# Attention's projections set ahead by a step or two, the feed-forward's weight preparation taken into attention, and a conditional pass put first

## The chip, the cores and the metric

The kernel runs on one core of a Trainium2 chip, as one program that is launched once. Five engines each work through a queue of their own, in order: PE (matrix multiplication, with PEld for its weight loads), DVE (vector), ACT (scalar functions), POOL (GpSimd) and SP (which here only starts DMAs). The metric is the device time of one execution in microseconds (us); four runs of the kernel before are given, and their median is what a time of the kernel after is held against.

## The reference

A two-layer block on 64 sequences of 64 tokens with 256 channels, 4096 tokens in all, in f32. Only the first layer's attention and feed-forward bear on the change:

```python
x = x + attn(cond(x, cond_1024), query_proj, key_proj, value_proj, output_proj)
x = x + ffn(cond2(x, cond_1024, weight), norm1_w, w1, act_scale, act_bias, norm2_w, w2)
# ... second layer: recurrent net, state-space scan, two mixtures of experts

def attn(x, ...):                  # 16 heads, keys of 16, values of 64
    q, k, v = x @ query_proj, x @ key_proj, x @ value_proj
    a = softmax(q k / sqrt(16), axis=1)
    return (a v) @ output_proj

def cond2(x, y, weight):           # y: one row for each sequence
    ys = y / sqrt(256)
    d = rsqrt((ys * ys) @ (weight * weight) + EPS)
    return (x * ys[:, None, :]) @ weight * d[:, None, :]

def weight_quant(w):               # in both products of ffn
    scale = 1.0 / clip(mean(abs(w)), 1e-5, None)
    return clip(round(w * scale), -1, 1) / scale
```

The feed-forward quantizes its activations too (root mean square, largest absolute value, rounding to 127 steps) and has relu squared between its two products. The conditioning `cond` ends with a projection whose bias is `bo`; in the data of this case `bo` is zero.

## The kernel before

**Stages.** The program goes through its stages one behind the other: a convolution and scan that make `cs`, what attention reads (`conditioned_scan`, L129, until about 146 us); `attention` (L301, to 431.6 us); `ffn0` (L486, to about 700 us); `rnn`, `mamba` with the first mixture beside it, and `mixtures`. The feed-forward's weights are loaded behind the scan (`ffn0_weights`, L449); further down SP's queue follow large fills of memory for the mixtures (`regions`) and copies of weights (`packed`), which keep the DMA engines busy from 100 to 340 us. The residual `xT` stays in the fast memory, with the channels on the partitions.

**Attention.** Rather than project values and outputs apart, the kernel multiplies `cs` as it stands by the attention weights and then by `M`, which is Wv times Wout, made by `value_weights` (L288: four times PE L297 into a bank, evicted by DVE). `keys` is `cs` transposed, 128 tokens by 128 (PE L317, evicted in turn by DVE and ACT).

`attend` (L330) goes over eight units (`NU`) of 512 tokens. A unit has four steps, (i, h) = (0,0), (0,1), (1,0), (1,1), here called A, B, C and D; a letter with a stroke (A') is a step's work done later. Each step has four parts:

- `scores`: eight matrix products q k on PE, each of several passes (L385), into two PSUM banks; for each bank DVE takes the maximum (L390) and subtracts it (L391); ACT takes exp of 128x1024 (L397); DVE the row sums z (L400) and their reciprocals; POOL multiplies E by them (L401).
- `follow`: a list, `late`, holds back the rest of a step until two more steps have been issued. Then `values` gives E times `keys` (PE L410) into two banks, which ACT copies to `oT` (L412).
- behind the fourth step's `values` `project_out` follows: two times eight products of 128x512 (L418) and an addition to `xT` on DVE (L420).
- `project_in(u+1)`, issued behind step D's scores: for q and then for k four products on PE (L359) into two banks, and their evictions, all on ACT: 16 for q (L367: masked by head and biased, 128x256) and four for k (L364).

PSUM has eight banks in two rings: "acc" (4) for `values`, `project_out`, M and keys; "ps" (4) for scores, q and k, which is why a product into a "ps" bank waits for the eviction of what was written four banks before. The scheduler builds each engine's queue from the order of issue and what each instruction waits for; so the first q and k, M and the keys are set beside the tail of the scan.

**The bias pass.** Where `bo` is not zero the same `attend` runs once more with a vector of biases in place of values. A count of nonzero entries, `wa.any`, is loaded into a register of each engine (L321) and a branch (L322) jumps over it, as it does with this data. It stands behind the main `attend`.

**The feed-forward's preparation.** `ffn0` begins with what depends on weights alone: `ternary` (L469) for w1 and w2 (a reduction of the absolute values L475, their sum over partitions by PE L477, the mean L478, its reciprocal L479, two passes over 128x2048, L480 and L481, and a cast, L482), a factor L506 for each, and for the conditioning `ys`, `ysq`, `wsq` (L509 to L513), four passes of a product (PE L516) and `rsqrt` (L89: a square root on ACT, then five DVE instructions L92 to L96). Then a software pipeline goes over 16 pairs of tiles of 128 tokens; its first stage, `product`, is xs on POOL (L562), PE L573 and L577, dt on ACT (L579) and gm on DVE (L580).

Of the kernel before, what the change touches and what calls it, by code (L numbers as in the profile page):

```python
# [300 lines left out]
def attention(g, wa, cs):  # L301
# [4 lines left out]
    nc, tc = g.nc, g.tc  # L306
    with tc.tile_pool(name="keys", bufs=1) as kp:
        M = kp.tile([P, wa.H // 2, D], F32, name="M")
        rows = kp.tile([P, NT // CH, 2, P], F32, name="keys")
        cs2 = cs.rearrange("p b l -> p (b l)")  # L310

        def before():
            value_weights(g, wa, lambda i, r: wa.Wv[r, i, :], M)
# [6 lines left out]
        attend(g, wa, cs2, lambda u, i: rows[:, u, i], M, before)  # L320
        for v in nc.values_load_multi_w_load_instructions(wa.any, min_val=0, max_val=D)[1]:  # L321
            with tc.If(v > 0):  # L322
                ones = kp.tile([P, P], F32, name="ones")
                nc.vector.memset(ones, 1.0)
                c = kp.tile([P, wa.H // 2, D], F32, name="c")
                bv = lambda i, r: wa.bv[r, i : i + 1].to_broadcast([L, L])
                attend(g, wa, cs2, lambda u, i: ones, c, lambda: value_weights(g, wa, bv, c, 1.0 / L))


def attend(g, wa, cs2, keys, M, before):  # L330
# [12 lines left out]
    with (  # L343
# [4 lines left out]
        def project_in(u):  # L348
# [5 lines left out]
            for i in range(2):  # L354
                ps = [bank(g, (P, 2, UT)) for _ in range(2)]
                for hg in range(2):
                    for h in range(2):
                        W = wa.Wqkv[half(h), i * HK + hg * P : i * HK + (hg + 1) * P]
                        nc.tensor.matmul(ps[h][:, hg, :], W, cs2[half(h), ts(u, UT)], start=True, stop=True)  # L359
                for h in range(2):  # L360
                    for hg in range(2):
                        if i:
                            b = wa.bqk[:, 1, hg : hg + 1]
                            nc.scalar.activation(v.k[:, hg, h, :], ps[h][:, hg, :], AF.Identity, bias=b)  # L364
                        else:
                            for j in range(4):
                                nc.scalar.activation(  # L367
                                    v.q[:, hg, h, :, j, :],
# [63 lines left out]
        for u in range(NU):  # L432
            for i in range(2):
                for h in range(2):
                    late.append((u, now, h, i, scores(now, h, i)))
                    if not (u or i or h):
                        before()
                    if i and h and u + 1 < NU:
                        now = project_in(u + 1)
                    if len(late) > 2:  # L440
                        follow()
# [1591 lines left out]
```

## Time and profile before

| what | us |
|---|---|
| four runs | 2945.47, 2947.01, 2947.2, 2950.5 |
| their median | 2947.11 |
| the profiled execution | 2955.37 |
| its span, first to last instruction | 2953.7 |
| attention's starts of L418, one for each unit | 183.27, 217.30, 251.24, 284.99, 318.39, 351.64, 385.78, 414.71 |
| attention's last addition to xT | 430.91, for 0.69 |
| the feed-forward's first gm | 456.31 |

Busy times over the whole span, and the first slices of 73.8 us each (a digit is the busy share in tenths; attention lies in slices 3 to 6, the feed-forward in 6 to 10):

```profile
PE 2421.3 (82%) x12134; PEld 1719.5 (58%) x12148; DVE 1756.8 (59%) x2955; ACT 1406.2 (48%) x2402; POOL 1306.2 (44%) x1117
## 2 busy tenths in 40 slices
PE   4978866778957788888787888868987899999996
PEld 4533323446824455555555565646875678888885
DVE  0454447884059997989887979895244343333232
ACT  0564435775366576767555666653422222222220
```

Read them thus: no engine is busy all the way, so the limits differ from stage to stage. In attention (third to sixth digit) PE has 6 to 8 tenths, ACT 3 to 6, DVE 4 to 5: something waits for something in each unit. How the rest is to be read (stretches, timelines, chains of waits) is told where it is used.

### The profile page before, as it was taken

Reading aid. Unit: us, or ns where it says so; the run is one execution under the profiler, and the core shown is the slowest. Engines: PE = TensorE matmul, PEld = TensorE weight load, DVE = VectorE, ACT = ScalarE, POOL = GpSimd, SP = SyncE. Lnnn points to the kernel's source line nnn. Section 1 sums busy time; section 2 is a strip of 40 time slices with the busy share of each in tenths; the row PEclk is TensorE's granted clock in tenths of the full one; section 3 lists DMA queues with packets and bytes.
Section 4 is the critical chain, followed back from the end, with each engine's and each line's share of the span. In section 5 each row is a group of like instructions: output and inputs, shape, how many; then the busy total and the mean of one; then the engine's idle time right before and its main releaser. Section 6 shows DMA issues by size and latency. Waiting matters only on the chain.

```text
span 2953.7 us, 34689 instructions
## 1 busy us (share of the span) xinstructions
PE 2421.3 (82%) x12134; PEld 1719.5 (58%) x12148; DVE 1756.8 (59%) x2955; ACT 1406.2 (48%) x2402; POOL 1306.2 (44%) x1117
## 2 busy tenths in 40 slices
PE   4978866778957788888787888868987899999996
PEld 4533323446824455555555565646875678888885
DVE  0454447884059997989887979895244343333232
ACT  0564435775366576767555666653422222222220
POOL 0022214552056767677757777773644441111110
PEclk9989987889767898999889999989998999999998
DMA  9999611000011222221212212222686856555655
GB/s 235 370 356 340 195 29 42 19 19 19 15 50 58 86 69 68 69 75 62 75 44 68 90 68 90 77 96 74 208 265 225 309 204 245 207 211 187 220 182 180
DMA packets 183075, 406.04 MB, mean 137 GB/s; under 512 B 25312, under 2 KB 89056, under 8 KB 177520
## 3 DMA queue, kind: packets, MB, share of 16 engines
q1 hardware_dynamic: 169456, 366.80, 37.0%
q0 software_dynamic: 13440, 36.98, 3.2%
q8 instruction: 97, 1.59, 0.2%
q14 instruction: 82, 0.67, 0.1%
HBM read 280.76 MB, written 144.98 MB: 144 GB/s over the span
## 4 chain that ended last, share of the span: by engine, by line
PE 43%; DVE 20%; ACT 9%; issue 6%; POOL 4%; DMA 2%; SPq 0%; DVEq 0%; ACTq 0%; POOLq 0%
DVE hb L954 11%; PE ps L1540 11%; PE acc L1438 8%; DVE hb L956 3%; PE ps L1507 2%; PE yp L970 2%; PE mq L1676 2%; PE mq L1692 2%; DVE xc L796 2%; PE mp L851 2%; PE ps L690 1%; PE ps L573 1%; POOL hb L915 1%; PE acc L690 1%; PE mp L789 1%
## 5 line engine op out<-in xcount | busy, mean ns | idle before, releaser
L915 POOL TENSOR_TENSOR hb<-dx,Bn 128x1024 f32<-128x1024 f32 x256 | 601.1, 2357 | 261.9 <-PE yp L970 256.0
L954 DVE TENSOR_TENSOR_SCAN hb<-dA,hb 128x512 f32<-128x512 f32 x512 | 602.9, 1209 | 32.5 <-ACT dA L922 29.9
L922 ACT ACTIVATE dA<-delta,A 128x504 f32<-128x504 f32 x512 | 344.3, 683 | 305.6 <-DVE hb L954 302.4
L970 PEld LDWEIGHTS yp<-ident,hb 128*128 128x128 f32 x2048 | 268.4, 152 | 180.6 <-issue 142.2
L956 DVE TENSOR_TENSOR hb<-hb,cb 128x1024 f32<-128x1024 f32 x256 | 312.1, 1219 | 83.0 <-PE cb L867 66.2
L1540 PE MATMUL ps<-gxT,w 128*128 128x256 f32 (+1 forms) x1600 | 325.9, 362 | 0.8 <-DVE gxT L1415 0.8
L1540 PEld LDWEIGHTS ps<-gxT,w 128*128 128x128 f32 x1600 | 277.1, 191 | 47.2 <-issue 12.1
L970 PE MATMUL yp<-ident,hb 128*128 128x128 f32 x2048 | 302.7, 292 | 0.0
L1676 PE MATMUL mq<-x,moe_s 128*128 128x256 f32 x896 | 250.4, 412 | 49.1 <-ACT up L1683 28.4
L1222 POOL DMA_INDIRECT ffn_y<-gy,to x72 | 69.3, 962 | 457.9 <-ACT gy L1440 445.9
L1676 PEld LDWEIGHTS mq<-x,moe_s 128*128 128x128 f32 x896 | 169.3, 204 | 113.9 <-ACT up L1683 37.1
L1544 DVE TENSOR_TENSOR gh<-gs,ps 128x256 f32<-128x256 f32 (+1 forms) x200 | 78.8, 394 | 219.2 <-ACT gs L1543 219.1
L867 PE MATMUL cb<-parts,pick 80*128 80x512 bf16 x256 | 105.4, 412 | 111.0 <-DVE hb L956 95.8
L1438 PE MATMUL acc<-w,gh 128*128 128x256 f32 (+1 forms) x864 | 187.6, 387 | 0.0
L1543 ACT ACTIVATE gs<-ps 128x256 f32<-128x256 f32 (+1 forms) x200 | 72.6, 363 | 233.2 <-PE ps L1540 229.2
L1440 ACT ACTIVATE gy<-acc,wt 128x256 f32<-128x256 f32 x152 | 67.1, 473 | 241.6 <-PE acc L1438 230.2
L401 POOL TENSOR_TENSOR E<-E,z 128x1024 f32<-128x1024 f32 x32 | 60.8, 1901 | 250.2 <-DVE z L400 250.2
L1438 PEld LDWEIGHTS acc<-w,gh 128*128 128x128 f32 (+1 forms) x864 | 145.6, 189 | 29.9 <-issue 12.8
L1692 PE MATMUL mq<-moe_s,sh 128*128 128x256 f32 x448 | 116.7, 399 | 6.6 <-ACT up L1683 6.6
L418 PE MATMUL acc<-oT,M 128*128 128x512 f32 x256 | 114.2, 605 | 7.8 <-ACT oT L412 7.6
L1222 POOL DMA_INDIRECT moe_y<-gy,to x80 | 77.1, 964 | 80.4 <-ACT gy L1440 61.3
L1692 PEld LDWEIGHTS mq<-moe_s,sh 128*128 128x128 f32 x448 | 83.8, 197 | 42.4 <-issue 20.2
(459 smaller groups left out, 4493.4 us busy)
## 6 DMA issues: line engine op xcount, KB each, us to landing
w<-ffn_w SPq DMA_DIRECT2D x40, 2176.0 KB, 9.3
Bn<-B SPq DMA_DIRECT2D x128, 512.0 KB, 3.6
moe_x<-fill SPq DMA_DIRECT2D x130, 260.0 KB, 5.8
ffn_x<-fill SPq DMA_DIRECT2D x129, 260.0 KB, 5.9
w<-moe_w SPq DMA_DIRECT2D x48, 512.0 KB, 4.6
ffn_w<-in_ffn_W_dram SPq DMA_DIRECT2D x16, 640.0 KB, 8.4
gx<-moe_x SPq DMA_DIRECT2D x32, 260.0 KB, 4.5
gx<-ffn_x SPq DMA_DIRECT2D x32, 260.0 KB, 9.4
```

Of the source, the lines that this page charges most:

```text
L418: nc.tensor.matmul(ps, M[:, o, ts(k, P)], v.o[:, o], start=(o == 0), stop=(o == H // 2 - 1))
L867: nc.tensor.matmul(t, pick[:, n : n + 1].to_broadcast([rows, P]), v.parts, start=True, stop=True)
L915: nc.gpsimd.tensor_mul(hb, vs[c].dx[p], Bn[:, n % NB, :].unsqueeze(1).to_broadcast([P, PI, CH]))
L922: nc.scalar.activation(decays[s][i][:, :, 1:], seq(vs[c].delta[p][:, i, :])[:, :, 1:], AF.Exp, scale=w.A[:, p * PI + i, n : n + 1],)
L954: ins = nc.vector.tensor_tensor_scan(h, dA[i].rearrange("p b l -> p (b l)"), h, 0.0, ALU.mult, ALU.add)
L956: ins = nc.vector.tensor_tensor(hb, hb, cb.unsqueeze(1).to_broadcast([P, PI, CH]), ALU.mult)
L970: nc.tensor.matmul(yp[i][:, t, :], hb[:, i, ts(t, P)], g.ident, start=(n == 0 and t == 0), stop=(n == S - 1 and t == CH // P - 1), is_tran ...
L1222: i = self.g.nc.gpsimd.indirect_dma_start(out=self.y, out_offset=bass.IndirectOffsetOnAxis(ap=to, axis=0), in_=y, in_offset=None)
L1438: nc.tensor.matmul(po[s], h, w, start=(i == 0), stop=(i == n - 1))
L1540: nc.tensor.matmul(ps[:, j, :], v.w12[:, k, ts(j * (full + 1) + i, P)], v.xT[:, k, :], start=(k == 0), stop=(k == KD - 1))
L1676: nc.tensor.matmul(ps[:, i % 2, :], w[:, k, ts(i, P)], xu[:, k, :], start=(k == 0), stop=(k == KD - 1))
L1692: nc.tensor.matmul(ps[:, t, :], h[:, i, ts(t, P)], self.s2[:, i, :], start=(i == 0), stop=(i == NS - 1))
```

## The change

Three things are done. Line numbers in what follows are those of the kernel before; in the kernel after the same lines of `attend` stand two further down, those of `ffn0` 25.

1. **q and k ahead.** `project_in` becomes `unit` (the tiles) and `project(u, v, i)` (q for i=0, k for i=1). The next unit's q is issued behind step B, its k behind step C, where both stood behind step D. The tiles, their buffers (two) and the banks stay.
2. **The preparation beside attention.** `ternary` returns its two results and a generator of six pieces for each weight; `ffn0_prepared` adds two more (squares; product and sum) and the root, `last`. `attend` runs one piece behind each step's scores: first M and the keys, then w1's six, w2's six, the squares, the sums, each behind a step of its own, so until unit 3; the root comes when all steps have been issued, but takes its place in the queues where the scheduler sets it. The prepared tiles have a pool of their own, open over both stages.
3. **The bias pass first.** The register's load and the branch now stand in front of the main `attend`, with a pool of their own.

In the queues of the built program: the reductions L475 for both weights, ys, ysq and wsq stand on DVE between the scan's instructions. The first q and k, M and the keys, which stood beside the scan's tail, stand behind the branch. q of unit u+1 is projected by PE between the scores of steps B and C, k between C and D, and a part of step D's scores stands ahead of `project_out` of the unit before. w1's passes stand in unit 1, w2's in unit 2, sums and root in unit 4, ahead of step D's exp. ACT has three more table loads in the feed-forward's start. SP issues the loads of the router's weight, its bias and the shared experts' weights behind the feed-forward's first stores, and 45 small POOL memsets come behind its start. From the feed-forward's first pairs on, the queues are the same.

```diff
-def attention(g, wa, cs):
+def attention(g, wa, cs, beside):
...
+    (some,) = nc.values_load_multi_w_load_instructions(wa.any, min_val=0, max_val=D)[1]
+    with tc.If(some > 0), tc.tile_pool(name="bias", bufs=1) as kp:
...
+        attend(g, wa, cs2, lambda u, i: ones, c, iter([lambda: value_weights(g, wa, bv, c, 1.0 / L)]), [])
...
-        attend(g, wa, cs2, lambda u, i: rows[:, u, i], M, before)
-        for v in nc.values_load_multi_w_load_instructions(wa.any, min_val=0, max_val=D)[1]:
-            with tc.If(v > 0):
...
+        first = (lambda: value_weights(g, wa, lambda i, r: wa.Wv[r, i, :], M), keys)
+        attend(g, wa, cs2, lambda u, i: rows[:, u, i], M, chain(first, beside[0]), beside[1])
...
-        now = project_in(0)
+        nxt = unit()
+        for i in range(2):
+            project(0, nxt, i)
         for u in range(NU):
+            now, nxt = nxt, unit() if u + 1 < NU else None
             for i in range(2):
                 for h in range(2):
                     late.append((u, now, h, i, scores(now, h, i)))
-                    if not (u or i or h):
-                        before()
-                    if i and h and u + 1 < NU:
-                        now = project_in(u + 1)
+                    for piece in islice(beside, 1):
+                        piece()
+                    if nxt and i != h:
+                        project(u + 1, nxt, i)
                     if len(late) > 2:
                         follow()
+        for piece in chain(beside, last):
+            piece()
         while late:
             follow()
...
+    def pieces():
+        yield lambda: nc.vector.tensor_reduce(s[:, 0:1], w, AX.XY, ALU.add, apply_absolute_value=True)
...
+        yield mean
+        yield lambda: nc.vector.tensor_scalar(w, w, s[:, 1:2], MAGIC, ALU.mult, ALU.add)
+        yield lambda: nc.vector.tensor_scalar(w, w, MAGIC, 1.0, ALU.subtract, ALU.min)
+        yield lambda: nc.vector.tensor_scalar(wq, w, -1.0, None, ALU.max)
+        yield lambda: nc.vector.tensor_scalar(s[:, 0:1], s[:, 0:1], 1.0 / 127.0, None, ALU.mult)
+
+    return wq, s[:, 0:1], pieces()
...
+    def squares():
+        nc.vector.tensor_scalar(ys, g.condT, 1.0 / math.sqrt(D), None, ALU.mult)
+        nc.vector.tensor_mul(ysq, ys, ys)
+        nc.vector.tensor_mul(wsq, w.Wc, w.Wc)
+
+    def sums():
+        ps = bank(g)
+        for k in range(KD):
+            nc.tensor.matmul(ps[:B, :D], ysq[:, k, :], wsq[:, k, :], start=(k == 0), stop=(k == KD - 1))
+        nc.vector.tensor_scalar(d2[:, 0, :], ps[:B, :D], EPS, None, ALU.add)
+
+    return chain(one, two, (squares, sums)), (lambda: rsqrt(nc, d2[:, 0, :], d, d2[:, 1, :]),)
...
+    p_ffn0, close_ffn0 = scoped(tc, "w_ffn0", side="right")
+    attention(g, w_attn, cs, ffn0_prepared(g, p_ffn0, w_ffn0))
     close_attn()

     ffn0(g, w_ffn0)
+    close_ffn0()
```

## The prediction, made before the result was known

> **What bounds the kernel now.** I read the utilisation by slices first, then the stretches the change touches. The profiled execution took 2955.37 us (span 2953.7, plus 1.7 around it); the median of the four runs is 2947.11, so 8.3 us are taken off at the end. Attention runs from 146 to 431.6 us, the first feed-forward from there to about 700. Behind the feed-forward's first pairs the built program puts the same instructions in the same order on all five queues, so nothing after 700 us gains or loses by itself: what attention and the feed-forward's start save, the whole saves.
>
> One unit of attention in two stretches (us, then busy us of PE, PEld, DVE, ACT, POOL, clock, DMA share, GB/s), the output projection of L418 and all the rest:
>
> ```profile
> 251.20:265.20 14.00, 13.96 (x36) 6.03 (x36) 3.81 (x7) 1.06 (x1) 3.80 (x2) 1.00 1.01 375
> 265.20:285.00 19.80, 14.04 (x114) 6.90 (x113) 12.87 (x20) 15.90 (x31) 3.80 (x2) 0.91 0.94 302
> ```
>
> PE fills the first; in the second PE works 14.04 of 19.80 and ACT 15.90. ACT's timeline of that second stretch:
>
> ```profile
> 266.79 1.07 ACT L412 COPY oT<-acc 128x512 f32<-128x512 f32 x2 [12.79 <-PE acc L410]
> 268.45 1.06 ACT L397 ACTIVATE E<-E 128x1024 f32<-128x1024 f32 x1 [0.59 <-DVE E L391]
> 269.42 2.37 ACT L367 ACTIVATE q<-ps,bq,mask 128x256 f32<-128x256 f32 x5
> 272.23 1.06 ACT L397 ACTIVATE E<-E 128x1024 f32<-128x1024 f32 x1 [0.44 <-DVE E L391]
> 273.19 5.11 ACT L367 ACTIVATE q<-ps,bq,mask 128x256 f32<-128x256 f32 x11
> 278.13 1.63 ACT L364 ACTIVATE k<-ps,bqkv 128x256 f32<-128x256 f32 x4
> 279.56 2.14 ACT L412 COPY oT<-acc 128x512 f32<-128x512 f32 x4
> 282.92 1.06 ACT L397 ACTIVATE E<-E 128x1024 f32<-128x1024 f32 x1 [1.23 <-DVE E L391]
> 283.89 1.06 ACT L412 COPY oT<-acc 128x512 f32<-128x512 f32 x2
> ```
>
> ACT is full from 268.45 to 281.7. What waits for it is PE, whose scores (L385) stand behind the last k:
>
> ```profile
>   ACT k L364: 72.0, 26
> ```
>
> These 72.0 us are PE's and its weight loads' idle time together; of PE alone 31.9 in 8 waits. Between the starts of two output projections lie 33.75 us (251.24 to 284.99; the others 33.25 to 34.1, the last, without a next unit's q and k, 28.9).
>
> The second place is the seam, in the chain of waits (start, us, what):
>
> ```profile
> 432.70 1.77 issue
> 434.47 2.29 DVE w1s L475
> 436.75 2.19 DVE w2s L475
> ...
> 440.65 1.98 DVE w L480
> ...
> 448.07 1.97 PE ps L516 x4
> 450.04 5.24 PE ps L573 x16
> 455.28 0.60 PE ps L577 x4
> 455.91 0.38 ACT dt L579
> 456.31 0.43 DVE gm L580
> ```
>
> From attention's last addition (431.62) to the feed-forward's first product (456.31) lie 24.69 us of preparation that nothing covers.
>
> **The change, part by part**
>
> *The seam.* Reductions, ternary weights, squares, sums and root go in front. What stays behind the last matmul (430.91): POOL's xs, 1.04; four passes of the product at 0.33 (5.24/16), 1.3; L577 0.6; dt 0.38: first product at about 434.3 in place of 456.31, **-22.0**. If xs takes the 2.1 it shows beside DVE and eight passes stand before dt, -19.5; if xs starts under the last matmuls, -23.1.
>
> *Table loads at the seam.* ACT's queue gains three in the feed-forward's start: a load took 1.28 each time it shows, so **+2.5**, between 0 (hidden behind POOL and DVE) and 3.85.
>
> *The branch moves* to 146 us. Before, all engines reach it at their own time; its rows:
>
> ```profile
> L322 PEldq COMPARE_BRANCH  x1: 3385/3385/3385, 423.6 to 423.6; - x1
> L322 DVEq COMPARE_BRANCH  x1: 72/72/72, 431.5 to 431.5; - x1
> ```
>
> [...] My own sum takes: PE and ACT reach the branch well before cs is done (their next work needs cs, 145.55), so 3.4 is hidden; DVE, last, pays its release, 0.6 (72 ns, then 21 ns at 432.2 after 431.5); bounds 0 and 3.4, DVE's 2.87 of idle before L475 between them. What stood beside the scan's tail (M, keys, first q and k, 136 to 144) now comes behind the branch: a table load, 1.28, stands ahead of the first q; M's four evictions fall behind the reductions that moved into the scan (two of 2.28, hidden but for 1.0) and that about cancels. **+1.8** (0 to +7).
>
> *The first unit.* In after, ACT's queue from the first q to the oT that the first output projection needs holds three units' q (48 at 0.47, 22.6), two units' k (8 at 0.41, 3.3), six exp (1.03 each, 6.2), eight oT (0.53, 4.2) and the keys (four, 2.3): 38.6, with four waits of about 1 (they were 0.57 to 2.59 in this stretch of before) 42.6. Before, with one q less, it was 37.6 (145.64 to 183.27). **+5.0** (+1 to +8).
>
> *Five steady periods.* The order after, from one output projection's end: ACT does two oT (done 1.3 later, as PE's four L410 come first), exp (4.35), four oT (6.3), exp (9.3), six q (12.3), exp (13.3), ten q (18.0), two oT (19.0); k is evicted under the projection. Then 14.0: 33.05 in place of 33.75, **-0.7 each, -3.5**. The wait for k goes, and ACT's own queue, with the 16 q still ahead of the last oT, is late next. Bounds: ACT's work alone in that list, 3 exp, 8 oT, 16 q = 14.8 behind PE's 1.3, gives 30.1 (-3.65); a stretch of 25 gives 39.0 (+5.3).
>
> *The unit without q and k.* The next-to-last projection's stretch carried the q and k of the last unit; now q comes a period earlier: 14.0+10.7 (8 oT, 3 exp and their waits of the last period before) = 24.7 against 33.3, **-8.6** (-5 to -9).
>
> *Pieces inside attention.* w1's two passes and cast (L494, L495: 1.28 or 2.06 by L480's rows below, 1.22 each) stand in DVE's queue ahead of unit 1's maxima and subtractions, which exp and PE's banks wait for; DVE is busy 12.87 of 19.80, so most is hidden: +1. w2's: +0.7. The root in unit 4 puts two table loads and a sqrt (3.0) ahead of an exp on ACT, behind a 1.74 DVE row: +2, as ACT has no slack there. **+3.7** (0 to 17.3, all of it uncovered: w1 and w2 9.0, root 4.4, tables 3.0, small ones 0.9).
>
> ```profile
> L480 DVE TENSOR_SCALAR w<-w,w1s x1: 2059/2059/2059, 440.6 to 440.6; 128x2048 f32<-128x2048 f32 x1
> L480 DVE TENSOR_SCALAR w<-w,w2s x1: 1280/1280/1280, 443.8 to 443.8; 128x2048 f32<-128x2048 f32 x1
> ```
>
> The slower one ran beside POOL's xs. [...]
>
> *Queues passed.* SP's loads of Wr, the router's bias and the shared weights move behind the feed-forward's stores, and 45 small POOL memsets behind its start: their readers run after 700 us, nothing.
>
> *Sum.* -22.0+2.5+1.8+5.0-3.5-8.6+3.7 = -21.1: profiled 2934.3, median **2926**.
>
> **Rivals**
>
> *R1, more.* With k off its path ACT runs its list without waits: periods of 30.1 (-14.7 on five), and pieces and seam loads cost nothing (-6.2): -42, **2905**. For it: ACT's 1.23 and 0.59 waits are small. Against: exp follows DVE, whose steps are spaced by PE's banks.
>
> *R2, the moved preparation lands on the path.* [...] For: ACT, the bound, gets the tables; against: DVE idles a third of each unit.
>
> *R3, slower.* Four PSUM banks are shared by scores, q and k. After the change the scores of the next unit stand in PE's queue ahead of an output projection, and their bank is free only when the q and k in it have been evicted; ACT evicts q after an exp. If this ring makes the stretch 25 us, five periods cost +5.3 each where I took -0.7: +30, so -21.1+30 = +9, **2956**. It decides from a stretch of 23.3 on (4.2 over my 19.05, five times 4.2 is the 21 gained); ACT's list with every wait of 31.9/8 = 4.0 added once gives 23.0.
>
> **How the numbers follow.** Forecast 0.62, R1 0.18, R2 0.12, R3 0.08. The forecast's own range, from the seam, the first unit and the pieces, is 2914 to 2939. The range of eight in ten takes in most of R1 and of R2: 2900 to 2944. About 0.2% (5.9 us) is what a measurement of this kernel can tell from no change; faster by more: 0.62+0.18 with a little of R2, 0.82; same 0.11; slower R3 with the rest, 0.07.
>
> **What would show it.** The feed-forward's first product 2 to 4 us behind attention's last addition, against 24.7: else the seam failed. "ACT k" gone from the waits of L385, starts of L418 33 us apart: 30 is R1, 36 and more, with PE waiting for ACT's q ahead of a projection, R3. The first projection at 188 to 190 us, against 183.27. The last two projections 25 us or less apart twice. DVE passes L494, L495 in units 1 and 2 with exp idle behind them by more than 5 us: R2. I am wrong if the branch at 146 us stops an engine for more than 4 us, or if the first projection is late by more than 8.

## The result, and the profile after

The kernel after takes 1.0024 times the kernel before (95% interval 1.0018 to 1.0031; medians 2959.02 us of 52 runs and 2949.15 of 78): 7 us slower, where 21 faster was forecast. Its profiled execution took 2956.04 (span 2954.2). That execution starts the state-space stage's first scan at 862.0 us, against 854.8 before: some 7 us are lost up to there, and all of what follows looks at that part. The two profiled executions end only 0.5 us apart, since the state-space stage, whose instructions didn't change, took 1158.7 us from its first scan to its last in the one and 1166.0 in the other (1156 to 1170 over all profiles here). So the medians say how large the loss is, and a profile, which is one execution, says only where in the first 862 us it lies.

By the terms of the forecast's sum, from the two profiles (us):

| term | forecast | measured | from |
|---|---|---|---|
| seam: last addition to first gm | -22.0 | -22.0 | 2.65 (458.99 to 461.64) against 24.69 |
| three table loads behind it | +2.5 | +1.8 | first gm to first scan, 400.3 against 398.5 |
| start behind the branch: first q | +1.8 | +7.4 | 153.04 against 145.64 |
| first q to first projection | +5.0 | +10.0 | 47.63 against 37.63 |
| five periods, with the pieces in them | -3.5 + 3.7 | +16.3 | 184.7 against 168.4 |
| the period without q and k | -8.6 | -6.6 | 27.51 against 34.14 |
| last period and last projection | 0 | +0.3 | 28.94 and 16.43, against 28.93 and 16.17 |
| sum | -21.1 | +7.2 | |

The seam, in the chain of waits of the kernel after (start, us, what): the chain goes from the last projection straight into POOL's xs.

```profile
441.83 16.44 PE acc L420 x32
...
458.34 1.05 POOL xs L587
```

So the part that was surest came out to the tenth. What took it back lies in attention. PE's waits in it, between 149 and 458 us (waiting line, releaser, us in all, times, longest):

```profile
PE ps L363 <- DVE E L393: 17.3, 14, 2.6
...
PE ps L363 <- DVEq L310: 12.4, 1, 12.4
```

Its costliest groups in attention, before (146 to 432 us) and after (146 to 459); behind the bars stand busy time and mean ns, then the idle time ahead of them and what ended it:

```profile
L418 PE MATMUL acc<-oT,M 128*128 128x512 f32 x256 | 114.2, 605 | 7.8 <-ACT oT L412 7.6
L385 PE MATMUL ps<-q,k 64*64 64x256 f32 x512 | 53.6, 485 | 34.5 <-ACT k L364 31.9 <-DVE E L391 2.6
...
L359 PE MATMUL ps<-cs,Wqk 64*128 64x256 f32 x112 | 23.7, 406 | 8.7 <-DVE E L391 8.4
```

```profile
L420 PE MATMUL acc<-oT,M 128*128 128x512 f32 x256 | 123.6, 644 | 1.2 <-ACT oT L414 1.2
L387 PE MATMUL ps<-q,k 64*64 64x256 f32 x512 | 63.1, 476 | 7.1 <-DVE E L393 4.5 <-ACT k L367 2.4
...
L363 PE MATMUL ps<-cs,Wqk 64*128 64x256 f32 x128 | 40.8, 546 | 31.1 <-DVE E L393 17.3 <-DVEq L310 12.4 <-ACT q L370 1.5
```

The wait for k fell from 31.9 to 2.4, as it should. But other waits grew (for a bank at q's and k's products from 8.4 to 17.3, for POOL's E at the products with the keys from 6.5 to 13.3), and PE got busier with the same work: the same 256 passes of the output projection take 9.4 us more; a pass of q's or k's product takes 546 ns instead of 406. (16 passes of L359 lay ahead of the window in the kernel before.) For the projections the reason stands in the clock column of the stretches; here one unit of the kernel after, projection and rest, to hold against the two lines at the head of the prediction:

```profile
241.83:257.57 15.74, 15.74 (x37) 6.71 (x39) 2.20 (x4) 1.46 (x4) 1.90 (x1) 0.89 0.97 359
257.57:277.73 20.16, 15.98 (x119) 8.84 (x118) 14.51 (x23) 15.49 (x29) 5.70 (x3) 0.79 0.96 324
```

Before, PE waited once, long (3.47 us, to 278.7); the clock fell to 0.50 behind that wait, from 279.2 to 282.6 us, and was back at 1.00 when the projection began, which took 14.00. After, the waits are short and many, the clock is 0.79 in the stretch, and the projection begins at half clock (0.50 until 245.4 us) and takes 15.74, which is 14.00 divided by its clock of 0.89. Over all of attention the mean clock is 0.81, against 0.91.

### The profile page after: what moved, and what is told of

Same layout as the page of the kernel before. It is cut to its first block, busy times and chain, and to the rows that moved or that the text cites. A ratio compares the mean times of both kernels' runs of the same rounds, so it can differ in the third digit from the quotient of the medians.

```text
span 2954.2 us, 34708 instructions
## 1 busy us (share of the span) xinstructions
PE 2440.0 (83%) x12134; PEld 1730.2 (59%) x12148; DVE 1764.0 (60%) x2955; ACT 1411.4 (48%) x2406; POOL 1304.8 (44%) x1117
## 4 chain that ended last, share of the span: by engine, by line
PE 42%; DVE 20%; ACT 9%; issue 7%; POOL 4%; DMA 2%; SPq 0%; DVEq 0%; POOLq 0%; ACTq 0%
DVE hb L979 12%; PE ps L1565 11%; PE acc L1463 8%; DVE hb L981 3%; PE ps L1532 2%; PE yp L995 2%; PE mq L1701 2%; PE mp L876 2%; DVE xc L821 1%; PE ps L715 1%; PE ps L598 1%; PE mq L1717 1%; PE acc L715 1%; PE ps L1573 1%; ACT dA L947 1%
## 5 line engine op out<-in xcount | busy, mean ns | idle before, releaser
L979 DVE TENSOR_TENSOR_SCAN hb<-dA,hb 128x512 f32<-128x512 f32 x512 | 602.8, 1209 | 34.6 <-ACT dA L947 32.1
L995 PEld LDWEIGHTS yp<-ident,hb 128*128 128x128 f32 x2048 | 267.0, 151 | 182.8 <-issue 144.2
L1701 PEld LDWEIGHTS mq<-x,moe_s 128*128 128x128 f32 x896 | 170.8, 206 | 114.4 <-ACT up L1708 36.8
L1463 PEld LDWEIGHTS acc<-w,gh 128*128 128x128 f32 (+1 forms) x864 | 145.6, 189 | 29.9 <-issue 12.8
L420 PE MATMUL acc<-oT,M 128*128 128x512 f32 x256 | 123.6, 644 | 1.2 <-ACT oT L414 1.2
L1717 PEld LDWEIGHTS mq<-moe_s,sh 128*128 128x128 f32 x448 | 81.5, 192 | 40.8 <-issue 18.0
```

The costliest lines, as they stand in the source:

```text
L420: nc.tensor.matmul(ps, M[:, o, ts(k, P)], v.o[:, o], start=(o == 0), stop=(o == H // 2 - 1))
L979: ins = nc.vector.tensor_tensor_scan(h, dA[i].rearrange("p b l -> p (b l)"), h, 0.0, ALU.mult, ALU.add)
L995: nc.tensor.matmul(yp[i][:, t, :], hb[:, i, ts(t, P)], g.ident, start=(n == 0 and t == 0), stop=(n == S - 1 and t == CH // P - 1), is_tran ...
L1463: nc.tensor.matmul(po[s], h, w, start=(i == 0), stop=(i == n - 1))
L1701: nc.tensor.matmul(ps[:, i % 2, :], w[:, k, ts(i, P)], xu[:, k, :], start=(k == 0), stop=(k == KD - 1))
L1717: nc.tensor.matmul(ps[:, t, :], h[:, i, ts(t, P)], self.s2[:, i, :], start=(i == 0), stop=(i == NS - 1))
```

## The experiments

Eighteen kernels were run, in five groups, each against the kernel before on the same chip. The theories (A the clock, B the pieces, C the branch; later P, R and S) are stated with the first run that tests them. On those chips the kernel before took 2958 to 3021 us; where it took over 3000, the runs' profiles are longer behind the state-space scan (from its last instruction to the first L1540, by the lines of the kernel before, 350 to 359 us against 314, and from there to the last L1540 582 to 587 against 564). So beside the ratio stands where the time before the state-space stage went: its first scan's start, from the profile (854.8 in the kernel before). This start carries what the end of the scan differs by (144 to 148 us, and 151 in the two runs with three banks), and a ratio carries the later stages, which vary by several us from run to run: where the two disagree, both are given.

| run | what it is | ratio (95%) | first scan | first projection | periods |
|---|---|---|---|---|---|
| before | | 1 | 854.8 | 183.3 | 34.0 33.9 33.8 33.4 33.3 34.1 28.9 |
| after | branch, q and k, preparation | 1.0024 (1.0018-1.0031) | 862.0 | 200.7 | 41.2 35.9 37.5 34.9 35.3 27.5 28.9 |
| e1_branch | branch alone | 0.9965 (0.9947-0.9983) | 846.5 | 190.7 | 33.2 34.1 34.1 34.1 34.1 34.0 32.4 |
| e2_qk | q and k alone | 1.0014 (0.9998-1.0029) | 860.0 | 192.4 | 33.0 35.1 34.6 33.7 33.0 28.1 29.0 |
| e3_prep | preparation alone | 0.9986 (0.9974-0.9998) | 852.0 | 184.6 | 34.1 35.3 36.6 35.0 33.2 34.1 28.9 |
| e4_no_branch | q and k, preparation | 1.0041 (1.0025-1.0057) | 867.0 | 197.0 | 42.1 35.4 36.6 35.0 33.0 28.1 29.0 |
| e11_no_qk | branch, preparation | 0.9969 (0.9955-0.9984) | 850.6 | 190.3 | 35.6 36.8 36.6 33.4 34.0 33.9 28.9 |
| e12_no_prep | branch, q and k | 0.9970 (0.9953-0.9986) | 845.1 | 194.0 | 36.6 34.0 34.1 34.1 34.1 26.8 33.0 |

These eight are all combinations of the three parts. With the branch in front, either of the other two is 9 us faster than before by the ratio (0.9970, 0.9969; by the first scan 9.8 and 4.2), which is no more than the branch alone gives; both together are 7 slower. **The loss is in the meeting of the two**: from e12_no_prep to the kernel after it is 16 us by the ratios (0.0054 of 2950) and 16.9 by the profiles. With the branch behind, too, the two together (1.0041) lose more than their single effects add up to (1.0014 and 0.9986).

### The parts alone

**e1_branch**, the branch moved in the kernel before:

```diff
+    (some,) = nc.values_load_multi_w_load_instructions(wa.any, min_val=0, max_val=D)[1]
+    with tc.If(some > 0), tc.tile_pool(name="bias", bufs=1) as kp:
...
     attend(g, wa, cs2, lambda u, i: rows[:, u, i], M, before)
-    for v in nc.values_load_multi_w_load_instructions(wa.any, min_val=0, max_val=D)[1]:
-        with tc.If(v > 0):
```

> The kernel before with the branch alone moved in front of attention. In the kernel after, DVE reached the branch at 145.5 us and came out of it at 149.4, and the first q was evicted 7.4 us later than before (153.04 against 145.64). Theory A (the clock: the new order of q and k scatters PE's waits, its clock falls to half more often, and that makes the loss): the branch alone costs these 7 us and gives 1 to 3 back at the seam, so 4 to 7 slower than before, with periods between output projections still 33.3 to 34.1. Theory B (the pieces on DVE make the loss): the same, 4 to 7. Theory C (the branch is the main loss; it also upsets what follows): 15 or more slower, with the first output projection at 198 or later.

It is 0.35% faster: all three theories missed it. Its own DVE timeline tells why. The preparation, whose text nobody moved, runs in attention's last unit, from here to 430.4 us:

```profile
389.02 2.29 DVE L475 TENSOR_REDUCE w1s<-w 128x1 f32<-128x2048 f32 x1 [4.89 <-ACT k L364]
```

The branch had been the wall that kept the scheduler from setting it there. First gm comes 2.8 behind the last addition; the last period is 3.5 longer (32.4), the first projection 7.4 later. So one line moved, the branch, gets most of what the hand-placed pieces were meant to get.

**e2_qk**, **e3_prep**, **e4_no_branch** (the kernel before with `project` issued as in the kernel after; the kernel after with q and k put back behind step D and the branch behind attention; the kernel after with the branch behind):

> The kernel before with q issued behind step B and k behind step C, and nothing else. Theory A (clock): periods of some 35 us against 33.75 (+1.3 in five periods), the output projections at a mean clock under 1.00 and 14.8 us or more instead of 14.0, the first unit 5 longer, the unit without q and k 6 shorter: 3 to 8 slower than before in all. Theory B (pieces): the order by itself does what was forecast, -0.7 a period, +5 at the first unit and -8.6 at the last but one: 5 to 8 faster, projections at 14.0. Theory C (branch): as B.

> The kernel after with q and k put back behind step D and the branch behind attention; only the preparation is beside attention. Theory A (clock): the seam's 22 us are kept and the pieces cost 2 to 6 in attention: 14 to 20 faster than before. Theory B (pieces): the passes of 2.1 to 2.7 us on DVE cost 15 or more: within 7 of before. Theory C: as A.

> The kernel after with the branch put back behind attention; q and k ahead and the preparation beside attention stay. Theory A (clock) and theory B (pieces): only the branch's 7 us come back, 1 to 3 of it lost again at the seam: within 4 of before, and projections still at 14.8 to 16.2. Theory C (branch): 15 or more faster than the kernel after, projections at 14.0.

e2_qk gives the clock its clearest witness, since it repeats one order of queues with two times. Two of its units, projection and then the rest, side by side:

```profile
328.85:342.85 14.00, 14.00 (x37) 6.07 (x40) 2.56 (x4) 2.31 (x5) 1.90 (x1) 1.00 0.89 276
342.85:361.89 19.04, 15.00 (x113) 8.35 (x113) 14.21 (x23) 15.39 (x29) 5.70 (x3) 0.84 0.01 4
225.39:241.46 16.07, 16.07 (x37) 6.85 (x38) 2.55 (x4) 1.43 (x4) 1.90 (x1) 0.87 1.00 373
241.46:260.51 19.05, 15.69 (x113) 8.06 (x112) 14.22 (x23) 15.39 (x29) 5.70 (x3) 0.82 0.96 357
```

The stretch behind the projection takes 19.04 and 19.05: what the forecast had worked out by hand (19.05), and where the projection runs at the full clock the period is 33.04, as forecast (33.05). The other unit loses 2.07 in the projection alone, at clock 0.87. Rows of the granted clock in steps of 1 us show it going to 0.50 behind stretches of 3 to 4 us in which PE was busy about half the time (246 to 249 us: 0.36, 0.19, 0.48, 0.76), and back to 1.00 after 3.4 to 13.7 us. e2_qk's first projection is 8 late against the scan's end, not 5; the longest spell at 0.50 lies in that stretch (161 to 175 us), but its share of the 8 isn't shown apart.

e3_prep missed its 14 to 20: 4 faster. Three causes: the pieces cost 6 in the periods of units 0 to 3; from the first gm to the first scan it takes 405.5 us, not 398.5 (the kernel after: 400.3); and the seam takes 7.5, not 2.7, as DVE reaches the branch last (438.9) and comes out at 441.8, and POOL's xs waits for that:

```profile
442.13 2.04 POOL L588 TENSOR_TENSOR xs<-xT,ys 128x512 f32<-128x512 f32 x2 [23.34 <-DVEq L323]
```

The second comes with the third: PE stood idle for 5 us at this seam, its clock is 0.50 for 23.9 us from 443.7 on, and the feed-forward's first four gm come 3.0 us apart, where the kernel after, whose PE is at full clock there, has them 1.7 apart. All six runs with the branch behind and the preparation in attention have both (seam 7.5 to 8.1, then 404 to 405.5).

e4_no_branch missed all three theories: it is no faster than the kernel after (1.0041 and 1.0025-1.0057, against 1.0024; its first scan is 5 later), where by theories A and B it should have gained the branch's 7.

### The pieces elsewhere, filler, banks

**e5_under**: branch behind, q and k behind step D, and the pieces held in place under the output projections (they are pinned behind the instruction issued before them on their engine; without that the scheduler moves them up).

```diff
             x = xh[:, k, :, ts(u, UT)]
+            for piece in islice(pieces, 2):
+                tc.keep_in_program_order(piece())
             nc.vector.tensor_add(x, x, ps)
```

> Branch behind attention, q and k behind step D as before; the preparation's passes and root are pinned on DVE's and ACT's queues under the output projections of units 0 to 3, two pieces ahead of each addition to xT, and their sums stand with M and the keys. Theory A (what costs in attention is PE's clock and what delays the scores; a piece under a projection costs nothing): output projections start as in the kernel before within 1.5 us, with 14.0 each, and the seam takes 7.5 as in the run with the preparation alone (DVE's jump of some 3 us is in it): 13 to 18 faster than before. Rival (the pieces cost wherever they stand, by contention): the periods with pieces are 1 to 3 longer, as there, and it is 3 to 8 faster.

Ratio 0.9954 (0.9940-0.9967), first scan 847.3, first projection 185.1, periods 33.4 33.2 34.1 34.1 34.1 34.1 28.9, all projections but the last 14.0: as theory A had it, in the units with pieces too. (13.6 faster by the ratio, as forecast, 7.5 by the first scan: seam and feed-forward's start lose as in e3_prep.) DVE's busy time in such a projection (218.46 to 232.46 us) is 8.67, against 3.8 before, and nothing comes later.

**e6_under_qk**, the same with q and k ahead from unit 1 on:

> The same with q issued behind step B and k behind step C from unit 1 on (unit 0 still projects unit 1's behind its step D). Theory A (clock): the first projection starts as in the kernel before; the next-to-last period is 6 shorter; the steady periods are 33.04 where the projection has the full clock and 34.6 to 35.1 where it starts at half: 15 to 24 faster than before, no more than 7 better than with q and k behind. Rival (order: the loss of q and k ahead lies in the queues, whatever the clock): all five periods 34.5 or more and the same time as with q and k behind, or worse.

0.9993 (0.9984-1.0002), first scan 859.1, first projection 193.7, periods 37.4 36.6 36.1 35.9 34.2 27.0 30.0, projections 14.9 to 16.3. Theory A missed; the rival's forecast came, but for one period (34.2): the new order loses 12 us against e5_under, and no projection keeps the full clock.

**e7_fill** and its control **e8_three** (q and k alone; filler behind the scores, 4, 3, 2 and 0 products by step, in one bank taken from the ring for values):

```diff
+            for _ in range(FILL[2 * i + h]):
+                nc.tensor.matmul(fill, v.k[:, 0, 0, :P], v.q[:, 0, 0, 0].rearrange("p j l -> p (j l)"), start=True, stop=True)
```

> The kernel before with q and k ahead (as in the second run) plus filler on PE: behind the scores of steps A, B and C four, three and two products of 128x256 of q and k into a PSUM bank that nothing reads; the ring for values and output has three banks in place of four. Theory A (clock): the filler keeps PE busy in the gaps, so its clock stays up: all output projections at 14.0 to 14.3 and all steady periods at 33.1 or less, attention 6 or more shorter than in the run with three banks and no filler. Rival (the order of the queues sets the loss; filler is only more work in front of q's and k's products): periods longer than without filler, by up to the 4 us of filler in a unit.

> The control for the filler: q and k ahead alone, with three banks in place of four in the ring for values and output. Theory A: like the run with four banks, periods of 33.0 to 35.1 with projections between 14.0 and 16.1 by the clock at which they begin; 0 to 10 slower than before. Rival (banks): periods of 36 and more.

1.0105 (1.0090-1.0119) and 1.0029 (1.0019-1.0039). Filler raised the clock of the stretches (0.90 to 1.00, against 0.87) and yet the periods grew from 34.0 to 37.7, by about the filler's 4 us, as the rival said: in this order PE's waits are too short to hide it (those for a bank at q's and k's products are at most 1.0 each in e8_three). As a test of the clock it decides nothing.

**e10_fill_wait** puts filler where it fits, into the old order's wait for k, in e5_under:

```diff
+                    if u and not (h or i):
+                        fill = bank(g, tag="acc")
+                        for _ in range(3):
+                            x = nc.tensor.matmul(fill, M[:, 0, :P], cs2[:, :CH], start=True, stop=True)
+                            tc.keep_in_program_order(x)
```

> The run with the pieces under the projections, and three products of 128x512 as filler on PE (2.6 us at full clock; nothing reads them) in the wait of 3.5 us that PE has for q's and k's evictions, so that nothing real is queued later. Theory A (clock): the clock after the wait stays at 1.00 and step A's and B's scores take 2 in place of 3.3: periods of 33.2 in place of 34.1, 3 to 7 faster. Rival (the clock isn't set by PE's own idleness): clock 0.91 or less in the stretches, periods unchanged or longer by the filler.

Here the filler decides. The stretch behind a projection (of 14.00 in both) in e5_under, then in e10_fill_wait:

```profile
299.83:319.95 20.12, 13.94 (x112) 6.40 (x112) 12.86 (x20) 15.87 (x31) 3.80 (x2) 0.92 1.01 318
```

```profile
265.48:284.72 19.24, 16.09 (x119) 7.00 (x119) 12.86 (x20) 15.88 (x31) 3.80 (x2) 1.00 0.93 300
```

PE does 2.15 more in it, for nothing, and the stretch is 0.88 shorter, since the scores behind the wait run at the full clock: periods 33.24, five of seven. In the fifth and the seventh unit the projection fell to 0.89 instead (15.7), so the whole moved by 1.3 in its profile, and the ratio is 0.9977 (0.9964-0.9989), no better than e5_under's 0.9954: the mechanism is shown, the gain isn't.

**e9_k_first** (e5_under with k projected and evicted ahead of q):

> The run with the pieces under the projections, and k projected and evicted ahead of q, both behind step D. Step A's scores (h=0) then need four evictions of k and the eight of q that hold h=0, not all twenty. Theory A (what a unit of the old order loses is the wait for the last eviction and the half clock that follows it): PE's wait of 3.5 in each unit falls under 1, scores run at the full clock, periods come from 34.1 to 30.5 to 32.5: 10 to 22 faster than the run with the pieces under the projections. Rival (ACT's list of 24 instructions bounds the stretch whatever the order): periods stay within 0.7 of 34.1 and the time within 5.

0.9958 (0.9944-0.9973), first scan 843.3, periods 33.4 33.4 33.4 32.9 33.3 33.2 28.6. Step A's scores start earlier, but the oT copies then stand behind sixteen q on ACT: ACT's list bounds the stretch. Theory A missed; the rival's time came (4 faster than e5_under in the profile, nothing by the ratio), its periods nearly: they fell by 0.7 to 1.2.

**e11_no_qk** and **e12_no_prep** fill the table above:

> The kernel after with q and k put back behind step D; the branch in front and the pieces beside the scores stay. Theory A (the order of q and k, with PE's clock and with no slack left for the pieces, is what loses): 6 to 12 faster than before. Theory B (the pieces' places lose by themselves): within 4 of before.

> The kernel before with the branch in front and q and k ahead; the preparation stands in the feed-forward's program text as before, and the scheduler may move it up to attention's last unit, as it did where the branch alone was moved. Theory A: the branch's 8 faster and the order's 5 slower: 0 to 7 faster than before. Theory B (pieces in their places lose, q and k ahead don't): 8 to 14 faster.

e11_no_qk met theory A by the ratio (9 faster; 4 by the first scan). e12_no_prep didn't: 9 faster is outside A's 0 to 7 and inside B's 8 to 14, though its projections (14.6 to 15.8 us) show A's clock. So neither theory holds alone: by the ratios the new order by itself, with the branch in front, loses next to nothing on balance, and so do the pieces by themselves.

### What in the preparation hurts the new order

All of these are the kernel after with one thing taken back; e18_both is the last two together. The pieces in `w.late` run at the head of `ffn0`.

```diff
 e13_short (twice, and the cast)
-        yield lambda: nc.vector.tensor_scalar(w, w, s[:, 1:2], MAGIC, ALU.mult, ALU.add)
+        yield lambda: nc.vector.tensor_scalar(w[:, 0, :64], w[:, 0, :64], s[:, 1:2], MAGIC, ALU.mult, ALU.add)
 e14_acc (three sums)
-            ps = bank(g)
+            ps = bank(g, tag="acc")
 e16_together
-        first = (lambda: value_weights(g, wa, lambda i, r: wa.Wv[r, i, :], M), keys)
+        first = (lambda: (value_weights(g, wa, lambda i, r: wa.Wv[r, i, :], M), keys()),)
 e17_root_late
-    return chain(one, two, (squares, sums)), (lambda: rsqrt(nc, d2[:, 0, :], d, d2[:, 1, :]),)
+    w.late = (squares, sums, lambda: rsqrt(nc, d2[:, 0, :], d, d2[:, 1, :]))
+    return chain(one, two), ()
```

> The kernel after with its six passes over the weights (two passes and a cast for w1 and for w2) cut to 64 of 2048 columns, in the same places of the queues; POOL fills the rest of the two results with zeros long before, so most of the feed-forward's weights are zero and the output isn't the reference's. Everything else of the kernel after stays: branch in front, q and k ahead, sums, root, tables. Theory P (the six passes' time on DVE, 12 us or so, delays what frees PE's banks in the new order, where nothing else is waited for): first projection and first two periods fall by 8 to 13 us in all, to those of the run without the preparation (first start 50 us behind the scan, period 36.6, then 34): 0 to 8 faster than before. Rival R (the sums' own banks: three more allocations turn the ring of four by one, so that q, k and scores meet in other banks): little changes, 4 or more slower than before.

> The kernel after with the three sums of the preparation taken from the ring of banks for values and output, so that the ring of four for scores, q and k isn't turned. Theory P: within 4 of the kernel after. Rival R: 6 or more faster than the kernel after, that is no slower than before.

> The kernel after with M and the keys as one piece behind the first scores, as before the change, in place of keys one step later; the pieces behind them move up by one step. Theory S (the loss is a sum of several pieces that each stand in the way): the first projection comes 4 to 5 earlier (50 us behind the scan in place of 55.4), the rest as in the kernel after: 3 to 5 faster than the kernel after. Rival (one thing, the passes' place in the first two units): no change within 1.5 at the first projection.

> The kernel after with squares, sums and root taken out of attention's pieces; they stand in the feed-forward's text, and the scheduler sets them in front of its end, in the last unit. Theory S: the period between the third and fourth projection falls from 37.5 (38.9 and 37.9 in the two runs before this) to 34 or 35, the last one grows by up to 3: 1 to 4 faster than the kernel after. Rival (root and tables cost nothing there): periods as in the kernel after.

> Both of these: only the passes over w1 and w2 and their two sums stay in the second and third unit. Theory S: the gains add up, 4 to 9 faster than the kernel after, between 2 slower and 3 faster than before; what is left against the run without the preparation's pieces (9.7 faster than before by its profile) is the passes and the two sums, about 7. Rival: no better than the better of the two.

| run | ratio (95%) | first scan | first projection | periods |
|---|---|---|---|---|
| e13_short | 0.9992 (0.9979-1.0004) | 857.8 | 199.3 | 38.2 35.2 37.9 35.1 34.0 26.8 29.9 |
| e14_acc | 1.0002 (0.9992-1.0011) | 859.1 | 198.8 | 37.5 35.8 39.0 35.4 34.2 27.1 30.0 |
| e16_together | 0.9997 (0.9983-1.0012) | 846.8 | 194.1 | 37.2 35.8 34.1 35.1 34.6 27.0 28.9 |
| e17_root_late | 1.0025 (1.0012-1.0038) | 856.9 | 199.9 | 40.8 35.8 34.1 34.1 34.1 26.8 29.9 |
| e18_both | 1.0003 (0.9990-1.0016) | 851.2 | 196.7 | 38.1 35.9 34.1 34.1 34.1 26.8 29.9 |

Neither the passes' time nor the banks alone make the 16 us. e13_short gains 9 against the kernel after by the ratio, 4 by the profile; its first projection and first two periods fall by 5, where theory P said 8 to 13. e14_acc gains 6.5 and 3: by the ratio that is what rival R said, by the profile what theory P said, so the banks' part stays open. e13_short also takes less away than it seems: the six passes took 13.0 us in the kernel after and still take 5.2. Three of the cut ones need 1.28 to 1.66 us where the others need 0.20; each began while POOL multiplied E and ended with it (to 187.42 here):

```profile
185.52 1.90 POOL L403 TENSOR_TENSOR E<-E,z 128x1024 f32<-128x1024 f32 x1 [2.98 <-DVE z L402]
```

```profile
185.81 1.66 DVE L495 TENSOR_SCALAR w<-w,w1s 128x64 f32<-128x64 f32 x1
```

In the kernel after, five of the six full passes begin beside that multiplication too and take 2.07 to 2.69 us, each until 1.08 us behind its end, where the sixth, beside nothing, takes 1.21: of DVE's 13.0 us, some 6 (13.0 less six times 1.21) come with POOL's multiplication.

The largest single step by the profile is the strangest: M and the keys in one piece, which only moves the rest up by a step. In the kernel after, w1's first two passes lie between the maxima and the subtractions of unit 1 (DVE's timeline):

```profile
186.12 2.69 DVE L494 TENSOR_SCALAR w<-w,w1s 128x2048 f32<-128x2048 f32 x1
...
191.78 2.07 DVE L495 TENSOR_SCALAR w<-w 128x2048 f32<-128x2048 f32 x1
193.77 0.68 DVE L393 TENSOR_TENSOR E<-ps,mx 128x512 f32<-128x512 f32 x1
```

The subtraction at 193.77 frees the bank for k's product (L363), which PE was waiting for. Some us earlier DVE had stood idle for 5.62, waiting for scores; in e16_together the same two passes fall into that time, and almost clear of POOL's multiplications (1.49, and the second, at 174.39, 1.23):

```profile
177.67 0.69 DVE L392 TENSOR_REDUCE mx<-ps 128x8 f32<-128x512 f32 x1 [5.62 <-PE ps L387]
```

```profile
172.86 1.49 DVE L494 TENSOR_SCALAR w<-w,w1s 128x2048 f32<-128x2048 f32 x1
```

Its first projection comes 6.6 earlier. Its third period is 34.1 too, as the scheduler also set the root elsewhere. e17_root_late takes the root out by itself: the third period falls from 37.5 to 34.1, as expected, but the ratio (1.0025) is the kernel after's, while the first scan is 5 earlier: ratio and profile disagree, and its gain isn't shown. e18_both is 6 faster than the kernel after, within theory S's range, and no better than e16_together (8), as the rival said. So several pieces each have their own place and price, as theory S had it, but the gains don't add.

### The best of it

**e15_front**: branch in front, pieces pinned under the projections, k ahead of q and both behind step D.

> All that helped together: the branch in front, the pieces pinned under the projections, k ahead of q and both behind step D. Worked out from the single runs: the start 7.4 later as with the branch alone, the seam 2.7 in place of 8.1, periods of 33.3, the last period 28.9 in place of 32.4: the first scan instruction of the state-space stage at 839 to 844 us (854.8 before; 843.3 with the branch behind), 11 to 16 faster than before. Rival (what the branch in front brings is only that the preparation may move, which the pieces under the projections already have): 4 or more slower than with the branch behind.

0.9944 (0.9932-0.9957), 16.6 us faster than before on its chip (medians 3000.39 and 3017.01); first scan 836.7, periods 33.5 32.9 33.3 33.2 32.9 33.1 28.6, seam 2.65, mean clock in attention 0.93. That is a little more than forecast, and the rival (slower than with the branch behind) missed. It beats both kernels, and e5_under does too.

## Why the prediction was wrong

**What held.** The seam (2.65 against 2.7 worked out), the table loads (+1.8 against +2.5), the unit without q and k in sign and most of its size (-6.6 against -8.6), the wait for k (31.9 to 2.4). Even the hand-played stretch of 19.05 is right, in e2_qk, where nothing else was changed.

**The step that failed** is the sum for the five periods, in both its terms: "-0.7 each" for the new order and "+3.7" for the pieces, of which "most is hidden". e12_no_prep has the new order and the branch in front without the pieces, and so measures the two apart: the order by itself makes the five periods 4.5 longer than before (172.9 against 168.4), not 3.5 shorter; the pieces make them another 11.8 longer (184.7) and the way from the first q to the first projection 5.8 longer (47.6 against 41.9). That is 17.6 for the pieces in place of 3.7. (e12_no_prep pays 4.0 for its preparation in the last period, which is why the net is less.)

**The steady periods.** "33.05 in place of 33.75" took the projection at 14.0, a row measured in an order where PE came to it at full clock. That the clock is part of the order's price was not in the sum: no term had it, though the clock column stood in the quoted lines. In the kernel after, the first seven projections cost 9.2 more (15.84, 15.74, 14.87, 14.88, 16.21, 15.64, 14.0), by the clock alone, for they wait for nothing inside. In e12_no_prep all of the 4.5 lies in the five projections (74.5 against 70.0); its stretches add up to what they were before. In the stretches the clock's share isn't shown apart from the waits'.

**The pieces.** "Most is hidden" was read from DVE's busy share of the old order (12.87 of 19.80). In the old order it is roughly so: 6 in e3_prep, where 3.7 was taken for the new order, and nothing at all where they stand under the projections. In the new order it is 17.6, close to the 17.3 that was named as its upper bound, the preparation on the path, as R2 had it: DVE's idle time had been the wait for k (before, DVE does nothing from 275 to 280 us while PE waits), which the other part of the change took away. That a pass takes longer beside POOL (2.06 against 1.28 in the prediction's two rows) got no term of its own; it is some 6 of the passes' 13.0 us. The term was worked out on the kernel before, and its cover was removed by the term beside it.

**The branch.** "+1.8", bounds 0 to 7, was 7.4, outside them. PE's and ACT's jumps were hidden as assumed; DVE's wasn't, and PE's first product of q waits for it (the 12.4 above):

```profile
L310 DVEq COMPARE_BRANCH  x1: 72/72/72, 145.5 to 145.5; - x1
L310 DVEq EVENT_SEMAPHORE  x1: 21/21/21, 149.4 to 149.4; - x1
```

3.9 of jump, 2.2 of q's first products at half clock (0.50 until 153.2 us), 1.3 of table load. PE was in its branch from 133.6 to 137.7, ACT from 140.9 to 144.2, before `cs` was done. So the branch took PE 4.0, ACT 3.3 and DVE 3.9 us, and POOL, at 98.7 us, 0.4; why some take so long no row shows. The prediction had 0.6 for DVE's jump, from its rows at the seam (431.5 to 432.2). And yet the branch's move is the best part of the change, by what it lets the scheduler do, which the prediction didn't ask. At the seam the same jump costs 4.8 (7.5 against 2.7), and the slower start behind it another 5.

**The first unit.** +10.0 for +5.0, and with the branch the first projection at 200.7 where 188 to 190 was named and more than 8 late was to mean wrong: of the +10.0, +8.2 is there in e2_qk, but with the branch in front, as in the kernel after, the order alone costs +4.2 (e12_no_prep), close to the forecast, and the other 5.8 came with the pieces. With M and the keys as one piece (e16_together) they are gone again.

**The rivals.** R1 didn't come. R2's preparation did land on the path, at a price of 17.6, but the passes' own time explains only a part of it, and that 17.6 is so near 17.3 is partly luck. R3 named the ring, and PE's waits for a bank at q's and k's products did rise (8.4 to 17.3 in attention), but turning the ring back (e14_acc) gained only 3 in the profile and 6.5 by the ratio. None of the rivals had the clock.

What stays open: how much of the 16 us is DVE's delay, how much the order of the banks and how much the clock that follows both; no run held the clock fixed in the new order, since e7_fill's filler stood in the way itself.

## What to carry to other kernels

A wait that is taken out of an engine's middle may be another engine's cover: work out each part of a change on the kernel that the other parts leave, not on the one before. Look at the granted clock of the stretch behind a change; here the order with the long waits for k (31.9 us in 8) kept a mean clock of 0.91 in attention, the kernel after, with its many shorter ones, 0.81; a duration copied from a row holds only at that row's clock (the projection's 14.00 at 1.00 became 15.74 at 0.89). Before placing work by hand in front of a barrier, see what the scheduler does when the barrier itself is moved.

## What the runs showed of the hardware that was not expected

In the clock records of the two kernels' profiles, before and after, every spell at 0.50 lasts 3.413 us or a whole multiple of it (6.83, 10.24, 13.65 and on, 128 spells between 100 and 2900 us), and within a profile the spells begin whole multiples of 3.413 us apart. In the kernel before five of them, about one to a unit, begin 34.13 or 34.14 us apart (176.75, 210.88, 245.02, 279.15, 313.28).

Steady periods come out at the same 34.1 us in kernels with different queues: 34.13, 34.13, 34.13, 34.14 in e1_branch, 34.13, 34.12, 34.14, 34.13 in e5_under, 34.00, 34.07, 34.10, 34.11 in e12_no_prep, 34.11, 34.13, 34.12 in e17_root_late, where single units at other clocks take 33.04 (e2_qk) or 33.24 (e10_fill_wait). Ten times the shortest spell of 3.413 is 34.13. That a period is drawn to a whole number of such spells fits these numbers, but not every order does it: the kernel before has 33.94, 33.75 and 33.39 among its periods, e9_k_first and e15_front 32.9 to 33.5. No run here sets the length of a spell, so it is an inference of the author's; if it holds, it would also say why small savings in a unit vanish.

DVE's passes over the weights took longer where they began while POOL multiplied E: 2048 columns, 1.21 us by themselves, took 2.07 to 2.69 and ended 1.08 us behind POOL in each of five passes (the kernel after); 64 columns, 0.20 by themselves, took up to 1.66 and ended with POOL (e13_short).
